# A graph attention layer: weighing ahead of the logits' transposes, and an older pair of blocks scaled ahead of the scans

## The chip, the cores and the metric

One core of a Trainium2 chip runs the kernel. The metric is the device time of one launch in microseconds (us). The profile is one execution recorded by the hardware profiler. Engines: PE is TensorE (matmuls, transposes), DVE is VectorE, ACT is ScalarE, POOL is GpSimd, SP is SyncE, which here only issues DMAs.

## The reference

There are 12,500 nodes with 256 features and 200,000 edges (src, dst), sorted by dst; 8 heads of 32.

```
h = relu(layernorm(x))
q, k, v = h @ Wq + bq, h @ Wk + bk, h @ Wv + bv          # 8 heads of 32
logits = einsum('ehd,ehd->eh', q[dst], k[src]) / sqrt(32)
expv = exp(logits - segment_max(logits, dst)[dst])
attn = expv / segment_sum(expv, dst)[dst]
agg = segment_sum(attn[:, :, None] * v[src], dst)
y = h + gelu(agg + h @ Wskip + bskip)
out = x + layernorm(y) * gamma + beta
```

## The kernel before

A first part makes the tables: h, k and v side by side (`kv_tab`), and q. A second part plans the walk over the edges. Both end near 395 us in the profile. The rest is the walk, and the change lies in it.

The edges are cut into 8 streams of 25,000. A step takes 383 edges of every stream, as K = 3 tiles of 128 edges; there are NST = 66 steps. The loop body numbered c holds work of several steps, and `keep` ties every instruction to the one before it on its own engine, so each engine runs in the order in which the code names the calls.

Work of a tile j of step c:
- `gather` (L1033, POOL): 8 indirect DMAs, one per stream, fetch k and v of 128 edges each, 24 a step. Six `kv` buffers hold two steps of tiles. `gather_next` puts them in four parts of two among DVE's work: the first part waits until its buffer is free, the other three wait for the latest DVE instruction named ahead of them.
- `hot_e` (L1050 on PE, L1052 on ACT) makes `to_e`, which spreads q from nodes to edges; six products a step, three in the middle of the body and three near its end. `hot_n` makes `to_n`, which sums edges into nodes.
- `spread` (L1073, PE): q of each edge, two halves. `times` (L1082, DVE): q times k. `total` (L1089, DVE): sums over each head, the logits `L`.
- `turn` (L1097, PE): transposes `L` into the PSUM tile `turned`. `maxima` (L1108, L1109, L1111, DVE): two scans along the edges of a stream, which need all three tiles turned, and a subtraction. `exponent` (L1115, ACT), `turn_back` (L1124, PE) puts the weights into other columns of the same tile `turned`.
- `weigh` (L1139, DVE): weight times v, into `vw`. It reads `turned`. `add_up` (L1163, PE; L1175 and L1181, ACT; L1185, SP) sums into nodes and stores the sums to `table` in DRAM.

A pair of 128-node blocks whose sums are complete is finished along the way, 46 of them in the loop, at most one begun in a step. `Pair` has these calls: `fetch` (six loads at L837: sums, x, h of two blocks), `turn` (L850 PE, L853 ACT), `divisors`, `divide` (L842 to L856, DVE), `skip` (L863, L867, PE), `add` (L872, PE), `gelu` (L876, ACT), `stats` (L879 to L885, DVE), `root` (L889, ACT), `factors` (L893, L894, DVE), `normal` (L899, ACT), `shifted` (L906, L909, PE), `scale` (L913, L915, DVE), `store` (L920, two stores by SP). The buffers of a pair are used again by the second pair after it.

In the body of step c, `pair` was fetched at the end of the body before; it goes as far as `gelu`. `before` is the pair of the previous body: it goes from `stats` to `store`. `pair_next` is fetched behind that store. Every load and store of a pair, the loads of q (`windows`, L1025, eight), `penalties` (L1011), `prefetch` (L1005) and the eight table writes (L1185) stand in SP's one queue in the order of the code.

Of the kernel before, what the change touches and what calls it, by code (L numbers as in the profile page):

```python
# [48 lines left out]
K = 3  # L49
# [710 lines left out]
def walk_streams(tc, N, HID, NST, KL, many, ident, idx, d0_row, slot_row, near, near_n, e_tab, pen_tab, h_tab,  # L760
# [48 lines left out]
    class Pair:  # L809
# [36 lines left out]
        def turn(self):  # L846
            ps = self.ps_h()
            for b in range(2):
                for c in range(KC):
                    self.keep(nc.tensor.transpose(ps[:, b, c, :], self.h[:, b, c * P:(c + 1) * P],  # L850
                                                  ident))
            self.hT = self.pool.tile([P, 2, KC, P], F32, name="hT", bufs=1)
            self.keep(nc.scalar.copy(self.hT, ps))  # L853
# [99 lines left out]
    with ExitStack() as es:  # L953
# [35 lines left out]
        def tiles_of(c):  # L989
            return KL if c == NST - 1 else K  # L990
# [36 lines left out]
        def gather(c, j, slots=range(S), behind=None):  # L1027

            if slots[0] == 0:
                step[c].setdefault("kv", []).append(gath.tile([P, S, KV], F32, name="kv"))  # L1030
            t = step[c]["kv"][j]
            for s in slots:
                ins = keep(nc.gpsimd.indirect_dma_start(  # L1033
                    out=t[:, s, :], out_offset=None, in_=kv_tab[:, :],
                    in_offset=bass.IndirectOffsetOnAxis(ap=idx[:, s, j, c:c + 1], axis=0)))
                if behind and s == slots[0]:
                    tc.add_manual_dep(ins.ins, behind, mybir.DependencyInfo(
                        mybir.DependencyClass.Sync, mybir.DependencyReason.DATA), reason="pace")

        def gather_next(c, j, part):  # L1040

            if 0 <= c < NST - 2 and j < tiles_of(c + 2):
                gather(c + 2, j, range(2 * part, 2 * part + 2), latest[DVE] if part else None)
# [22 lines left out]
        def spread(c, j, half):  # L1066

            g = step[c]
            ps = qe_ps.tile([P, 2, 2, HID], F32, name="ps_qe")
            for a in range(2):  # L1070
                for b in range(2):
                    i, at, w = rows_of(4 * half + 2 * a + b)
                    keep(nc.tensor.matmul(ps[:, b, a, :],  # L1073
                                          g["to_e"][at:at + w, i, j * P:(j + 1) * P],
                                          g["qw"][at:at + w, i, :], start=True, stop=True))
            g["qe", half] = ps
# [8 lines left out]
        def total(c, j):  # L1085
            g = step[c]
            if j == 0:
                g["L"] = work.tile([P, K, SH], F32, name="L")
            keep(nc.vector.tensor_reduce(g["L"][:, j, :].rearrange("p (s h) -> p s h", s=S),  # L1089
                                         g["kv"][j][:, :, :HID].rearrange(  # L1090
                                             "p s (h d) -> p s h d", h=HEADS),
                                         AX.X, OP.add))
# [9 lines left out]
        def maxima(c):  # L1102
            g = step[c]
            n = tiles_of(c) * P
            X, R, pen = turned[:SH, :n], turned[SH:, :n], g["pen"]
            M = g["M"] = work.tile([SH, CH], F32, name="M")[:, :n]
            W = g["W"] = work.tile([SH, CH], F32, name="W", bufs=1)[:, :n]
            keep(nc.vector.tensor_tensor_scan(R, pen[:SH, :n], X, -BIG, op0=OP.add, op1=OP.max))  # L1108
            keep(nc.vector.tensor_tensor_scan(mirrored(M, 0, n), mirrored(pen[SH:, :], 1, n),  # L1109
                                              mirrored(R, 0, n), -BIG, op0=OP.add, op1=OP.max))  # L1110
            keep(nc.vector.tensor_tensor(W, X, M, op=OP.subtract))  # L1111
# [23 lines left out]
        def weigh(c, j):  # L1135
            g = step[c]
            t = g["vw"][j]
            wj = weight(j)
            keep(nc.vector.tensor_tensor(  # L1139
                t[:, :, HEADS:].rearrange("p s (h d) -> p s h d", h=HEADS),  # L1140
                wj[:, :, :, None].to_broadcast([P, S, HEADS, D]),
                g["kv"][j][:, :, HID:].rearrange("p s (h d) -> p s h d", h=HEADS), op=OP.mult))
            if j == 0:
                keep(nc.vector.tensor_tensor(t[:, :, :HEADS], wj, wden[c % 2], op=OP.mult))  # L1144
# [96 lines left out]
                                  bank(i), keep))  # L1241
                lasts[i].fetch_rows()

        pair = before = None
        for c in range(NST - 1):

            pair_next = None
            if c in due:
                pair_next = Pair(fin, due[c][0],
                                 lambda: hot_ps.tile([P, 2, KC, P], F32, name="ps_hot"),  # L1250
                                 lambda: ag_ps.tile([P, 2 * HID], F32, name="ps_a").rearrange(
                                     "p (b d) -> p b d", b=2),
                                 keep)
            if c + 2 < NST:
                windows(c + 2)
            for half in range(2):
                times(c, K - 1, half)
                gather_next(c - 1, 1, 1 + half)
                spread(c + 1, 0, half)
            total(c, K - 1)  # L1260
            gather_next(c - 1, 1, 3)
            turn(c, K - 1)
            if c:
                weigh(c - 1, K - 1)
                gather_next(c - 1, K - 1, 0)
            maxima(c)
            gather_next(c - 1, K - 1, 1)
            if before:
                before.stats()
            if c:  # L1270
                add_up(c - 1, 0, range(K - 1, K))
                add_up_products(c - 1, 1)
            exponent(c)
            turn_back(c)
            if c:
                add_up_results(c - 1, 1)
            if c:
                add_up(c - 1, 2)
            carried(c)
            for half in range(2):  # L1280
                times(c + 1, 0, half)
                gather_next(c - 1, K - 1, 2 + half)
                spread(c + 1, 1, half)
            total(c + 1, 0)
            weigh(c, 0)
            gather_next(c, 0, 0)
            for j in range(K):
                hot_n(c, j)
            turn(c + 1, 0)
            if before:  # L1290
                before.root()
            if pair:
                pair.turn()
                pair.divisors()
                pair.divide()
                pair.skip()
            if before:
                before.factors()
            if c + 2 < NST:
                for i in range(QT // 2):  # L1300
                    hot_e(c + 2, i)
            if before:
                before.normal()
            if pair:
                table_of(AF.Gelu)
                pair.add()
                pair.gelu()
            if pair or before:
                table_of(AF.Exp)
            for half in range(2):  # L1310
                times(c + 1, 1, half)
                gather_next(c, 0, 1 + half)
                if tiles_of(c + 1) == K:
                    spread(c + 1, K - 1, half)
            total(c + 1, 1)
            gather_next(c, 0, 3)
            turn(c + 1, 1)
            if before:
                before.shifted()
            weigh(c, 1)  # L1320
            gather_next(c, 1, 0)
            if before:
                before.scale()
                before.store(0)
                before.store(1)
            if pair_next:
                pair_next.fetch()
            if c == NST - 2:
                for i in range(4):
                    last(i)  # L1330
            if c + 2 < NST:
                for i in range(QT // 2, QT):
                    hot_e(c + 2, i)
            add_up(c, 0, range(K - 1))
            if c + 2 < NST:
                penalties(c + 2)
            if c + 3 < NST:
                prefetch(c + 3)
            if c == NST - 2:
                weigh(c, K - 1)  # L1340
                add_up(c, 0, range(K - 1, K))
                add_up(c, 1)
                if pair_next:
                    pair_next.turn()
                    pair_next.skip()
            if c == NST - 2:
                add_up(c, 2)
            before, pair = pair, pair_next
            if c > 1:
                step[c - 2] = None  # L1350

        c = NST - 1
# [432 lines left out]
```

## Time and profile before

| | |
|---|---|
| median of 3 runs | 2546.08 us (2539.39 to 2546.2) |
| the profiled execution | 2542.74 us, span 2540.9 us |
| mean granted TensorE clock | 0.707 |
| busy: PE, DVE, ACT, POOL | 1772.4, 1998.0, 1081.4, 1659.9 us |
| DMA | 649.36 MB, mean 256 GB/s over the span |
| gathers by POOL (L1033) | 1576, 966 ns each |
| weigh on DVE (L1139) | 197, 2289 ns each |
| times (L1082), total (L1089) on DVE | 394 of 1217 ns, 197 of 2286 ns |

A row of the timeline has the start in us from the span's start, the duration, the engine, the line, the operation, output <- inputs, the shapes, the count, and in brackets the engine's idle time ahead of it with what ended it. A row of the list of waits has who waited, for whom, the total in us, how often, and the longest. "SPq" rows are SyncE's issues.

### The profile page before, as it was taken

How to read it: one execution, taken by the hardware profiler on the slowest of the kernel's cores; microseconds unless marked ns; L12 is line 12 of the kernel's file. 1: busy time of each engine (PE TensorE's matmuls, PEld its weight loads, DVE VectorE, ACT ScalarE, POOL GpSimd, SP SyncE). 2: the span in 40 equal slices, each digit the busy share in tenths (PEclk: the TensorE clock that was granted, in tenths of full speed). 3: DMA queues.
4: the chain of work that ended last, by engine and by line, in shares of the span. 5: the costliest groups of instructions: out<-in, count | busy, mean ns of one | idle time of the engine just before them, and what ended most of it. 6: DMA issues, size and time to landing. Idle time of an engine off the chain costs nothing. (4 is left out here: it accounts for less than half of the span.)

```text
span 2540.9 us, 29615 instructions
## 1 busy us (share of the span) xinstructions
PE 1772.4 (70%) x7824; PEld 926.5 (36%) x7824; DVE 1998.0 (79%) x2330; ACT 1081.4 (43%) x2459; POOL 1659.9 (65%) x1745
## 2 busy tenths in 40 slices
PE   6889974555567767667677677667777677676665
PEld 3445532222233333333333333333333333333333
DVE  7775946777788888888888888887877887888884
ACT  3333322333334545444444544444444444444443
POOL 3442447777777777677777677776776776776730
PEclk9999985666666766766676766676666766667677
DMA  7766678888898898888898898898887988988952
GB/s 249 272 227 248 256 256 247 255 260 258 254 278 256 270 281 254 267 276 260 252 279 272 252 280 265 262 278 256 264 267 242 290 253 244 293 255 257 291 169 79
DMA packets 306130, 649.36 MB, mean 256 GB/s; under 512 B 52836, under 2 KB 192238, under 8 KB 300954
## 3 DMA queue, kind: packets, MB, share of 16 engines
q0 software_dynamic: 128768, 423.23, 54.7%
q1 hardware_dynamic: 176434, 223.46, 26.7%
q8 instruction: 65, 1.06, 0.2%
q10 hardware_dynamic: 748, 0.66, 0.1%
q14 instruction: 115, 0.94, 0.1%
HBM read 538.91 MB, written 108.23 MB: 255 GB/s over the span
## 5 line engine op out<-in xcount | busy, mean ns | idle before, releaser
L1033 POOL DMA_INDIRECT kv<-kv_tab,idx x1576 | 1523.1, 966 | 567.9 <-issue 385.0
L1139 DVE TENSOR_TENSOR vw<-ps_x,kv 128x2048 f32<-128x2048 f32 x197 | 450.9, 2289 | 246.2 <-PE ps_x L1097 219.1
L1082 DVE TENSOR_TENSOR kv<-ps_qe,kv 128x1024 f32<-128x1024 f32 x394 | 465.4, 1217 | 84.0 <-DMA kv<-kv_tab,idx 82.0
L1089 DVE TENSOR_REDUCE L<-kv 128x64 f32<-128x2048 f32 x197 | 450.3, 2286 | 6.9 <-DVE kv L1082 0.2
L1163 PE MATMUL ps_a<-vw,to_n 128*32 128x264 f32 (+1 forms) x2344 | 304.5, 549 | 158.4 <-DVE vw L1139 158.4
L1073 PE MATMUL ps_qe<-qw,to_e 64*128 64x256 f32 (+1 forms) x1576 | 316.8, 400 | 111.2 <-DVE kv L1082 63.8
L1052 ACT ACTIVATE to_e<-ps_hot,ones 128x384 fp32r<-128x384 f32 x396 | 214.0, 576 | 364.1 <-PE ps_hot L1050 357.8
L1073 PEld LDWEIGHTS ps_qe<-qw,to_e 64*128 64x128 f32 (+1 forms) x1576 | 227.7, 253 | 281.6 <-DVE kv L1082 134.7
L1175 ACT COPY sums_w<-ps_a 128x264 f32<-128x264 f32 x130 | 49.3, 379 | 609.4 <-PE ps_a L1163 427.2
L1050 PE MATMUL ps_hot<-et,near 48*128 48x384 bf16 x396 | 150.6, 426 | 114.9 <-ACT to_e L1052 104.9
L1097 PE MATMUL ps_x<-ident,L 128*64 128x128 f32 x197 | 71.5, 363 | 210.6 <-DVE vw L1144 132.7
L1163 PEld LDWEIGHTS ps_a<-vw,to_n 128*32 128x32 f32 (+1 forms) x2344 | 103.2, 147 | 311.8 <-DVE vw L1139 189.1
L257 PE MATMUL ps_kv<-w_kv,hT 128*128 128x512 f32 x392 | 195.5, 621 | 16.0 <-ACT hT L142 14.8
L867 PE MATMUL ps_a<-w_s,hT 128*128 128x256 f32 x368 | 170.6, 644 | 50.3 <-ACT hT L853 49.6
L269 POOL TENSOR_TENSOR qp<-qp 128x256 fp32r<-128x256 f32 x98 | 88.4, 903 | 170.1 <-ACT qp L268 169.8
L1163 PE MATMUL ps_hot<-vw,to_n 128*64 128x264 f32 x808 | 187.6, 633 | 0.0
L867 PEld LDWEIGHTS ps_a<-w_s,hT 128*128 128x128 f32 x368 | 115.1, 328 | 94.4 <-ACT hT L853 69.6
L1181 ACT COPY kv<-ps_a 1x264 f32<-1x264 f32 x388 | 142.9, 368 | 6.3
L1097 PEld LDWEIGHTS ps_x<-ident,L 128*64 128x64 f32 x197 | 23.9, 121 | 310.3 <-DVE vw L1144 215.7
L987 ACT ACT_TABLE_LOAD x102 | 130.9, 1283 | 1.8
L1163 PEld LDWEIGHTS ps_hot<-vw,to_n 128*64 128x64 f32 x808 | 82.5, 219 | 109.2 <-issue 107.9
L263 PE MATMUL ps_q<-w_q,hT 128*128 128x256 f32 x392 | 104.1, 388 | 20.4 <-DVE qp L267 20.3
(278 smaller groups left out, 2110.3 us busy)
## 6 DMA issues: line engine op xcount, KB each, us to landing
qw<-q_pc SPq DMA_DIRECT2D x264, 128.0 KB
kv<-kv_tab,idx POOLq DMA_INDIRECT x1576
kv_tab<-kvo SPq DMA_DIRECT2D x16, 1280.0 KB
q_pc<-qp SPq DMA_DIRECT2D x16, 1280.0 KB
qw<-q_pc SPq DMA_DIRECT2D x264, 64.0 KB
table<-sums_w SPq DMA_DIRECT2D x264, 61.9 KB
pen<-pen_tab SPq DMA_DIRECT2D x66, 192.5 KB
sums<-table SPq DMA_DIRECT2D x92, 132.0 KB
```

The source lines that it names most:

```text
L257: ins = nc.tensor.matmul(ps_kv, hT[:, c, :], w_kv[:, c, :], start=c == 0, stop=c == KC - 1)
L867: self.keep(nc.tensor.matmul(self.ps[:, b, :], self.hT[:, b, c, :], w_s[:, c, :], start=False, stop=False, skip_group_check=True))
L987: keep(nc.scalar.activation(dummy[:, 1:2], dummy[:, 0:1], function))
L1033: ins = keep(nc.gpsimd.indirect_dma_start(out=t[:, s, :], out_offset=None, in_=kv_tab[:, :], in_offset=bass.IndirectOffsetOnAxis(ap=idx[:, ...
L1050: keep(nc.tensor.matmul(ps[:, :CH], near[:, i * P:(i + 1) * P], step[c]["et"], start=True, stop=True))
L1052: keep(nc.scalar.activation(step[c]["to_e"][:, i, :], ps[:, :CH], AF.Relu, scale=-1.0, bias=ones))
L1073: keep(nc.tensor.matmul(ps[:, b, a, :], g["to_e"][at:at + w, i, j * P:(j + 1) * P], g["qw"][at:at + w, i, :], start=True, stop=True))
L1082: keep(nc.vector.tensor_tensor(k, g["qe", half].rearrange("p b a d -> p a b d"), k, op=OP.mult))
L1089: keep(nc.vector.tensor_reduce(g["L"][:, j, :].rearrange("p (s h) -> p s h", s=S), g["kv"][j][:, :, :HID].rearrange("p s (h d) -> p s h d" ...
L1139: keep(nc.vector.tensor_tensor(t[:, :, HEADS:].rearrange("p s (h d) -> p s h d", h=HEADS), wj[:, :, :, None].to_broadcast([P, S, HEADS, D] ...
L1163: keep(nc.tensor.matmul(ps[at:at + w, :], g["to_n"][:, j, i * P + at:i * P + at + w], g["vw"][j][:, s, :], start=j == 0, stop=j == tiles_o ...
L1181: keep(nc.scalar.copy(step[c + 1]["kv"][0][0:1, s, HID - HEADS:], ps[at:at + 1, :]))
```

## The change

In the walk's loop: `weigh` of a tile stands directly behind the `total` of another tile, and the `turn` of that total behind it, at both places where it was the other way round. A pair is given a further body: `older` is the pair that was `before` a body earlier. `factors` and `normal` of `before` move behind the second `total`; `shifted`, `scale` and the two stores move into the next body, to `older`, `shifted` ahead of the first `total`, the others ahead of `maxima`. `fetch` moves from the end of a body to the next body, behind those stores. The last body does both at its end as before.

```diff
-        pair = before = None
+        pair = before = older = None
         for c in range(NST - 1):
...
                 times(c, K - 1, half)
                 gather_next(c - 1, 1, 1 + half)
                 spread(c + 1, 0, half)
+            if older:
+                older.shifted()
             total(c, K - 1)
             gather_next(c - 1, 1, 3)
-            turn(c, K - 1)
             if c:
                 weigh(c - 1, K - 1)
                 gather_next(c - 1, K - 1, 0)
+            turn(c, K - 1)
+            if older:
+                older.scale()
+                older.store(0)
+                older.store(1)
+            if pair:
+                pair.fetch()
             maxima(c)
...
                 pair.skip()
-            if before:
-                before.factors()
             if c + 2 < NST:
                 for i in range(QT // 2):
                     hot_e(c + 2, i)
-            if before:
-                before.normal()
             if pair:
                 table_of(AF.Gelu)
                 pair.add()
...
             total(c + 1, 1)
             gather_next(c, 0, 3)
+            if before:
+                before.factors()
+            weigh(c, 1)
+            gather_next(c, 1, 0)
             turn(c + 1, 1)
             if before:
-                before.shifted()
-            weigh(c, 1)
-            gather_next(c, 1, 0)
-            if before:
-                before.scale()
-                before.store(0)
-                before.store(1)
-            if pair_next:
-                pair_next.fetch()
+                before.normal()
             if c == NST - 2:
+                if before:
+                    before.shifted()
+                    before.scale()
+                    before.store(0)
+                    before.store(1)
+                if pair_next:
+                    pair_next.fetch()
                 for i in range(4):
                     last(i)
...
-            before, pair = pair, pair_next
+            older, before, pair = before if c < NST - 2 else None, pair, pair_next
```

## The prediction

> **What bounds the kernel now.** I read the list of waits first, because VectorE (DVE) has the largest share of the span (79%).
>
> ```profile
> DVE vw L1139 <- PE ps_x L1097: 219.1, 128, 5.4
> DVE rstd L893 <- ACT rstd L889: 65.0, 45, 2.9
> DVE kv L1082 <- DMA kv<-kv_tab,idx: 82.0, 30, 11.0
> POOL kv L1033 <- issue: 385.0, 1263, 0.3
> POOL kv L1033 <- DVE vw L1139: 75.5, 46, 3.4
> SPq L920 <- DMA out_dram<-o: 125.3, 48, 3.8
> ```
>
> Columns: total us, times, longest. DVE's largest wait is weigh (L1139) for a transpose of logits (L1097, turn). GpSimd's gathers mostly wait 0.3 us each, which is their own spacing.
>
> Next the timeline of one step, forward scan (L1108) to forward scan. DVE:
>
> ```profile
> 1535.61 0.96 DVE L1108 TENSOR_TENSOR_SCAN ps_x<-pen,ps_x 64x384 f32<-64x384 f32 x1
> 1546.53 0.21 DVE L1144 TENSOR_TENSOR vw<-ps_x,wden 128x64 f32<-128x64 f32 x1
> 1548.98 0.17 DVE L893 RECIPROCAL rstd<-rstd 128x2 f32<-128x2 f32 x1 [1.14 <-ACT rstd L889]
> 1551.78 2.29 DVE L1089 TENSOR_REDUCE L<-kv 128x64 f32<-128x2048 f32 x1
> 1558.96 2.29 DVE L1139 TENSOR_TENSOR vw<-ps_x,kv 128x2048 f32<-128x2048 f32 x1 [4.90 <-PE ps_x L1097]
> 1567.75 2.29 DVE L1139 TENSOR_TENSOR vw<-ps_x,kv 128x2048 f32<-128x2048 f32 x1 [0.52 <-PE ps_x L1097]
> ```
>
> TensorE (PE) in the same stretch:
>
> ```profile
> 1549.47 3.78 PE L867 MATMUL ps_a<-w_s,hT 128*128 128x256 f32 x8 [1.61 <-ACT hT L853]
> 1554.76 2.07 PE L872 MATMUL ps_a<-o,ident 128*128 128x256 f32 x4
> 1556.76 1.95 PE L1073 MATMUL ps_qe<-qw,to_e 64*128 64x256 f32 x8
> 1558.51 0.41 PE L1097 MATMUL ps_x<-ident,L 128*64 128x128 f32 x1
> 1559.39 2.08 PE L909 MATMUL ps_hot<-x_f,ident 128*128 128x256 f32 x4
> ```
>
> The transpose that weigh waits for is late because PE is late: it stands behind skip (L867), three to_e products, add (L872) and spread (L1073). So removing DVE's wait exposes PE next. SyncE:
>
> ```profile
> 1528.21 3.64 SPq L920 DMA_DIRECT2D out_dram<-o  x2
> 1532.51 0.35 SPq L837 DMA_DIRECT2D sums<-table  x1
> 1535.50 0.38 SPq L837 DMA_DIRECT2D h<-h_tab  x1
> ```
>
> The second store waits until the first has landed, and the fetch comes behind both.
>
> The scans' start times give step lengths. Steps 2 to 10, without pairs, average 30.3 us and wait some 5 us each for gathers. Steps 12 to 63 take 1684 us, 32.4 each. By content: 24 steps A (a pair computed, an earlier one finished, an older one to come; 19 of about 34.4, 5 of 32.4), 10 B (no older pair yet; nine of 32.2, one of 34.6), 9 C (no pair computed; 30.6), 9 D (a pair computed, none in normalisation; five of 30.5, four of 29.0). The clock separates the long and the short ones: the windows show PE granted 0.50 from 1548 to 1575, where the eight spread products take 1.95 us, and 1.00 from 1521 to 1527, where they take 1.17.
>
> **GpSimd's floor.** A gather takes 966 ns (page) plus 385.0/1263 = 0.305 us spacing; 24 per step make 30.5 us. No step can be shorter on average. Steps 0 to 10 stand there already, so I count nothing for them, nor for the first 395 us and the tail behind step 64, whose order is nearly the same.
>
> **Part by part, for step A**, in us from the scan start, 1535.61 as zero.
> - Weigh ahead of turn: takes away 4.90 + 0.52 of DVE wait. The transposes now stand behind weigh: 0.31 to start plus 0.42. The first is waited for only a step later; the second stands ahead of the scans, where the two scaling operations (0.68 + 0.69) cover 0.73. Without an older pair it costs that 0.73.
> - Factors later: the 1.14 wait (2.35 in C) goes, since the root ends at 13.3 and factors now come at about 17. The two normal activations (1.08) move behind ACT's Gelu and Exp loads, ahead of the last three to_e reliefs: PE's sixth to_e product waits for them.
> - Shifted, scale and stores one step later: as many instructions. Shifted (0.60 + 2.08, or 0.38 + 1.13 at full clock) now stands in PE behind spread, ahead of the last transpose, and scale's second half needs it.
> - Fetch: same six DMAs, but in the step that uses them. On SyncE they move from ahead of pen, et and the eight window loads to behind the two stores and ahead of the eight table writes. The first table write now waits for both sums to land, with half a step to spare. The window loads no longer queue behind the stores; they start when PE has done the last spread and take 6.59, so SyncE is free about 1 (full clock) to 3 us (half) before the stores.
>
> When do rows land? From the end of scale: last h issued at +7.3 (1535.50 - 1528.19). In the trace's release times h lands 6.03 after its issue (median of 26; 5.06 to 8.01), sums 5.58 (5.22 to 6.15). The store's landing is 3.16 in the median (1.72 to 4.72). So h lands between 10.9 and 16.9; I take 14.0, a little above the medians' 13.3, because window loads now stand just ahead in SyncE's queue. Sums land near 12.5, DVE wants them at 11.06 (A) or 9.4 (D): it waits 1.5 to 3, but PE's chain hides that. For h, hT is copied at 14.5 to 15.05 instead of 13.24 to 13.80: 1.25 late, the rest hidden by ACT's root.
>
> The Trainium skill, "DMA: Bandwidth & Descriptors", section "Anatomy of one DMA", gives, fitted for transfers that GpSimd issues, about 2.0 us plus bytes/436e3, an estimate of 2.3 us for these 128 KB; the trace has 6.03. By the rule nothing would be late and the sum would fall to the GpSimd floor.
>
> Chain of A at half clock: hT 15.05; skip, to_e and add end 7.4 later (as now, 13.80 to 21.2): 22.45; Gelu 0.57, Exp load and dummy 1.5, normal 1.08, relief 0.58: 26.2; sixth product 0.4, sums 1.99, spread 1.95, shifted 2.68, scale 0.69: 34.0. DVE alone would be there at 31. So **34.1** against 34.4: nearly all of the 5.4 reappears behind PE. At full clock (rows of the step at 1503: 5.94 from hT to add; 0.57, 1.48, 1.08, 0.56; 0.33, some 1.2, 1.17, 1.51, 0.69) PE ends at 29.6 and DVE at **29.9**, against 32.4.
> B has its rows early (no store before them): 1.25 less, and no more than that: 32.8 or 28.6. C loses 2.35 and 1.5 and gets the scaling it has today: 27.0 to 28.5, I take 27.5. D gains nothing at ACT, pays the late rows and 0.73 ahead of the scans: 31.3 or 29.1, a little worse than now.
>
> Sum with each step's clock as it is now: 19 x 34.1 + 5 x 29.9 + 9 x 28.6 + 32.8 + 9 x 27.5 + 5 x 31.3 + 4 x 29.1 = 1608. C, D, B in a row would ask their gathers in 28.4 to 29.1 each, under the floor by 4 to 6 us per group, of which the six kv buffers lend most: I add 10 for nine groups. 1684 - 1618 = 66 us. The profiled execution took 2542.7 (span 2540.9 and 1.8 around it; 3.3 under the median of the runs): **2477**, I say 2475. About 0.3%, 7.6 us, is what a measurement can tell from no change.
>
> **The clock.** The Trainium skill, "TensorE: Matmul & The Clock Gate", Part 1, says the clock halves after an idle window of about 3.4 us and returns after a busy one. The rows have 0.50 for 27 us in which PE's longest idle is 2.4, so the measurement decides. By the rule alone most steps would run at full clock, near 2445; but a wait for h beyond 15 would itself make a 3.4 us gap, which speaks against the change.
>
> **Rivals.**
> 1. GpSimd becomes the bound: PE gets warmer because its 2.38 us gap before the last sums goes. 52 x 30.5 = 1586: 98 less, 2445. For: the POOL row; against: half clock in most pair steps.
> 2. The rows come too late. Place: h for PE's transposes (L850) in the 33 steps A and D, each 1:1. Every us beyond 14.0 costs 33; at 2.0 beyond (16.0) the gain is gone; at 17 to 18 it is 2576 to 2609. For: landing rows to 8.01, window loads close ahead of the stores; half clock in B and C as well (10 x 4 and 9 x 1) does the same. Against: medians.
> 3. PE's own order gives everything back (A and B at half clock throughout, C as taken, rows on time): 24 x 34.1 + 10 x 32.8 + 9 x 27.5 + 9 x 31.3 = 1676, with the 10 no change: 2543 to 2546.
>
> **Chances.** Forecast (2455 to 2500) 0.45; rival 1 0.20; rival 2 0.25; rival 3 0.10, of which 0.03 falls on the faster side and 0.01 on the slower. Faster 0.68, same 0.06, slower 0.26. Range 2437 to 2557: from rival 1's end to the beginning of rival 2.
>
> **What the profile after would show.** Right: L1139's wait for L1097 under 20 us; L893's wait near nothing; new waits of L842 for sums and of L850 for h of 1 to 3 us in A and D; L915 waiting for PE; L1050 waiting longer for ACT; C under 29, A at half clock near 34. Wrong: waits for h over 4 us (rival 2), or GpSimd with hardly any wait but its 0.3 (rival 1).

## The result and the profile after

The changed kernel takes 2443.9 us (median of 4 runs, 2443.03 to 2448.57), the kernel before 2546.14 beside it: a ratio of 0.961, 95% interval 0.959 to 0.963. The profiled execution has a span of 2441.2 and takes 2443.03, 99.7 less than that of before. By the scans' start times, 97.5 of this lie in the 52 steps 12 to 63 (1684.3 before, 1586.8 after), 1.4 ahead of the first scan, 1.1 in steps 0 to 11; behind step 64 it is 0.3 longer.

The list of waits of the whole execution, after:

```profile
POOL kv L1033 <- issue: 357.8, 1174, 0.3
PE ps_x L1097 <- DVE vw L1139: 118.9, 57, 3.8
DVE kv L1082 <- DMA kv<-kv_tab,idx: 131.5, 64, 11.6
DVE kv L1082 <- PE ps_qe L1073: 77.0, 38, 3.5
DVE o L915 <- PE ps_hot L909: 47.8, 26, 3.5
PE ps_hot L850 <- DMA h<-h_tab: 37.0, 36, 2.5
DVE den L842 <- DMA sums<-table: 26.7, 29, 2.5
```

The wait of weigh (L1139) for the transposes (L1097), 219.1 us before, is gone from the list; now the transposes wait for weigh. The wait of factors for the root (L893, 65.0) is down to 2.8. New are waits for a pair's rows (L842, L850) and for its scaling product (L915), and VectorE's wait for gathered rows is longer than before (131.5 against 82.0).

The list of waits again, GpSimd alone, in the walk's 52 steps only. Before (759 to 2443.6):

```profile
POOL kv L1033 <- DVE vw L1139: 74.3, 42, 3.4
POOL kv L1033 <- DVE kv L1082: 44.0, 74, 2.4
```

After (757 to 2344):

```profile
POOL kv L1033 <- issue: 283.2, 929, 0.3
POOL kv L1033 <- DMA kv<-kv_tab,idx: 35.0, 115, 0.3
POOL kv L1033 <- DVE vw L1139: 5.8, 19, 0.3
```

The last column is what counts. Before, GpSimd stood up to 3.4 us for buffers that VectorE had not freed; over the steps 85 us lay beyond its own spacing. After, not one gather waits longer than 0.3, whoever is named: GpSimd issues without a break. Its cadence (the time from one gather's start to the next) is 0.965 + 0.305 = 1.27 us there, and 52 x 24 x 1.27 = 1585; the steps take 1586.8.

A view by windows has, for each stretch, each engine's busy time with the instructions in brackets, the clock, the DMA share and GB/s. The 52 steps after:

```profile
757.00:2344.00 1587.00, 1130.80 (x5482) 593.54 (x5476) 1374.93 (x1349) 798.30 (x1749) 1206.03 (x1250) 0.72 0.89 281
```

Before, the same stretch of work took 1684 with a granted clock of 0.67. By kinds of step:

| | forecast | measured (least to most) | clock before, after |
|---|---|---|---|
| A, 24 steps | 34.1 (19 of them), 29.9 (5) | 31.5 (30.3 to 33.7) | 0.67, 0.73 |
| B, 10 | 32.8 (1), 28.6 (9) | 31.7 (30.3 to 32.7) | 0.71, 0.73 |
| C, 9 | 27.5 | 27.8 (26.3 to 30.8) | 0.61, 0.66 |
| D, 9 | 31.3 (5), 29.1 (4) | 29.3 (27.7 to 31.4) | 0.70, 0.73 |

The longest step A after begins its scan at 1368.67 and takes 33.74. VectorE:

```profile
1386.69 2.29 DVE L1139 TENSOR_TENSOR vw<-ps_x,kv 128x2048 f32<-128x2048 f32 x1
1392.08 2.37 DVE L1082 TENSOR_TENSOR kv<-ps_qe,kv 128x1024 f32<-128x1024 f32 x2 [3.11 <-PE ps_qe L1073]
1401.81 0.69 DVE L915 TENSOR_TENSOR o<-sums,ps_hot 128x512 f32<-128x512 f32 x1 [2.25 <-PE ps_hot L909]
```

TensorE and GpSimd in it:

```profile
1382.59 0.69 PE L850 MATMUL ps_hot<-ident,h 128*128 128x128 f32 x2 [1.54 <-DMA h<-h_tab]
1383.95 3.78 PE L867 MATMUL ps_a<-w_s,hT 128*128 128x256 f32 x8
1391.24 1.94 PE L1073 MATMUL ps_qe<-qw,to_e 64*128 64x256 f32 x8
1399.70 2.08 PE L909 MATMUL ps_hot<-x_f,ident 128*128 128x256 f32 x4
```

```profile
1385.56 0.95 POOL L1033 DMA_INDIRECT kv<-kv_tab,idx  x1 [0.30 <-issue]
1389.34 0.95 POOL L1033 DMA_INDIRECT kv<-kv_tab,idx  x1 [0.30 <-DVE vw L1139]
```

Weigh no longer waits, and its 4.90 us have gone to TensorE as forecast: 3.11 at the next times, because skip (L867, 3.78 at half clock) holds the spread back, and 2.25 at the scaling. The last h lands 13.8 behind the end of the previous scaling (1382.59 - 1368.76). So this step is the forecast's A at half clock, 33.7 against 34.1. But GpSimd goes on through it at its cadence, into buffers freed earlier, and the short steps behind it catch up: the next one, a C, takes 27.2.

### The profile page after: what moved, and what is told of

It is laid out like the page before. It is cut to its first block, busy times and chain, and to the rows that moved or that the text cites. A ratio compares the mean times of both kernels' runs of the same rounds, so it can differ in the third digit from the quotient of the medians.

```text
span 2441.2 us, 29592 instructions
## 1 busy us (share of the span) xinstructions
PE 1707.4 (70%) x7824; PEld 908.6 (37%) x7824; DVE 1983.1 (81%) x2330; ACT 1086.9 (45%) x2459; POOL 1654.2 (68%) x1745
## 3 DMA queue, kind: packets, MB, share of 16 engines
q1 hardware_dynamic: 176434, 223.46, 27.2%
## 4 chain that ended last, share of the span: by engine, by line
PE 24%; DMA 23%; DVE 19%; issue 12%; POOL 11%; ACT 7%; SPq 2%; DVEq 0%; another core or an unknown queue 0%; ACTq 0%; POOLq 0%
DMA kv<-kv_tab,idx 15%; POOL kv L1033 10%; DVE vw L1139 5%; PE ps_a L867 5%; PE ps_kv L257 5%; DVE kv L1082 5%; DMA h<-h_tab 4%; DVE L L1089 3%; PE ps_q L263 3%; PE ps_qe L1073 3%; DMA out_dram<-o 2%; PE ps_a L1163 2%; ACT L987 2%; PE ps_a L872 2%; PE ps_hot L1050 1%
## 5 line engine op out<-in xcount | busy, mean ns | idle before, releaser
L1082 DVE TENSOR_TENSOR kv<-ps_qe,kv 128x1024 f32<-128x1024 f32 x394 | 469.0, 1218 | 213.3 <-DMA kv<-kv_tab,idx 131.5
L1139 DVE TENSOR_TENSOR vw<-ps_x,kv 128x2048 f32<-128x2048 f32 x197 | 449.5, 2282 | 15.4 <-ACT vw L1133 15.4
L1073 PE MATMUL ps_qe<-qw,to_e 64*128 64x256 f32 (+1 forms) x1576 | 313.4, 397 | 101.8 <-DVE kv L1082 98.2
L1073 PEld LDWEIGHTS ps_qe<-qw,to_e 64*128 64x128 f32 (+1 forms) x1576 | 224.8, 250 | 268.6 <-DVE kv L1082 156.6
L1163 PE MATMUL ps_a<-vw,to_n 128*32 128x264 f32 (+1 forms) x2344 | 283.1, 511 | 3.3 <-DVE vw L1139 3.3
L1097 PE MATMUL ps_x<-ident,L 128*64 128x128 f32 x197 | 73.4, 373 | 270.4 <-DVE vw L1144 145.2
L1050 PE MATMUL ps_hot<-et,near 48*128 48x384 bf16 x396 | 145.2, 427 | 126.2 <-ACT to_e L1052 121.7
L867 PE MATMUL ps_a<-w_s,hT 128*128 128x256 f32 x368 | 172.7, 649 | 20.9 <-ACT hT L853 17.5
L1163 PEld LDWEIGHTS ps_a<-vw,to_n 128*32 128x32 f32 (+1 forms) x2344 | 101.7, 140 | 202.9 <-issue 165.1
L1097 PEld LDWEIGHTS ps_x<-ident,L 128*64 128x64 f32 x197 | 25.1, 127 | 365.7 <-DVE vw L1144 221.3
L1163 PE MATMUL ps_hot<-vw,to_n 128*64 128x264 f32 x808 | 141.8, 500 | 0.9 <-DVE o L915 0.6
L867 PEld LDWEIGHTS ps_a<-w_s,hT 128*128 128x128 f32 x368 | 115.5, 329 | 69.3 <-ACT hT L853 44.2
L1063 ACT ACTIVATE to_n<-ps_hot,ones 128x384 f32<-128x384 f32 x197 | 104.0, 582 | 31.8 <-PE ps_hot L1061 31.0
```

What stands on the lines that cost most here:

```text
L867: self.keep(nc.tensor.matmul(self.ps[:, b, :], self.hT[:, b, c, :], w_s[:, c, :], start=False, stop=False, skip_group_check=True))
L1050: keep(nc.tensor.matmul(ps[:, :CH], near[:, i * P:(i + 1) * P], step[c]["et"], start=True, stop=True))
L1073: keep(nc.tensor.matmul(ps[:, b, a, :], g["to_e"][at:at + w, i, j * P:(j + 1) * P], g["qw"][at:at + w, i, :], start=True, stop=True))
L1082: keep(nc.vector.tensor_tensor(k, g["qe", half].rearrange("p b a d -> p a b d"), k, op=OP.mult))
L1139: keep(nc.vector.tensor_tensor(t[:, :, HEADS:].rearrange("p s (h d) -> p s h d", h=HEADS), wj[:, :, :, None].to_broadcast([P, S, HEADS, D] ...
L1163: keep(nc.tensor.matmul(ps[at:at + w, :], g["to_n"][:, j, i * P + at:i * P + at + w], g["vw"][j][:, s, :], start=j == 0, stop=j == tiles_o ...
```

## The experiments

**Theory:** in the changed kernel's walk GpSimd's issuing of gathers ends last, 30.5 us a step, and the swap of weigh and turn is what brought the other engines under it. **Rivals:** the pair's move did it; late rows of the pair still cost; transfers, or the chain of VectorE and TensorE, end at 30.5 by coincidence.

The runs fell on several chips. On one the kernel before takes 2541 us, nearly as in the first comparison; on three others it takes 3165, 3165 and 3214. There TensorE stands still at times with no releaser in the record, which is not explained, and ratios alone are compared.

**The changed kernel again**, no edit (on the chip with 2541).

> The changed kernel once more, on the chip of these runs, so that the others have it beside them. Where the kernel before takes 2546 us, both theories expect 2444. On a chip as in the runs before this one, where it takes about 3165 us because TensorE stands still with no releaser in the record: weighing ahead of the turn alone was worth a ratio of 0.964 there and the pair's move alone 0.9935, so their sum is 0.958; the theory of GpSimd's floor (30.5 us a step) expects between 0.955 and 0.965, as steps of 40 us do not touch that floor. The rival, that the pair's move is what mattered, expects that the two together are far below 0.95.

2447.84 us (2444.19 to 2449.32), ratio 0.963 [0.961, 0.965]. The 52 steps take 1590.8, again without a gather of GpSimd that waits longer than 0.3.

**h fetched early** (same chip).

```diff
-                self.rows_of(self.h[:, b, :], h_b, rows[b], HID)
+        def fetch_h(self):
+            self.h = self.pool.tile([P, 2, HID], F32, name="h")
+            rows = loaded(slot_row[0:1, self.m, 0:2], (N - P) * BX)
+            for b in range(2):
+                self.rows_of(self.h[:, b, :], h_b, rows[b], HID)
...
                 if pair_next:
                     pair_next.fetch()
+            if pair_next:
+                pair_next.fetch_h()
```

> The changed kernel, but the loads of h are issued at the end of the body before, where all six loads of a pair stood in the kernel before; sums and x stay at the new place. Theory of GpSimd's floor: h's wait (81 us in the trace of after, over PE and its weight loads) lies under the floor; where the kernel before takes 2546 us the time is that of the changed kernel, 2444, within 0.3 percent. Rival, late rows are what is left of the cost: 33 steps get up to 2.9 us each back, so 2444 less 40 to 80. On a chip where the kernel before takes 3165: in the trace there h was waited for 1 us in all, so no change beside the changed kernel.

2452.66 us (2450.79 to 2454.53), against 2447.84 for the changed kernel beside it: not faster by 40 to 80, but 5 slower (0.2%). The list of waits (lines stand 4 lower in this kernel: L846 is L842, L854 is L850, L1086 is L1082):

```profile
DVE den L846 <- DMA sums<-table: 9.9, 13, 1.6
PE ps_hot L854 <- DMA h<-h_tab: 1.8, 1, 1.8
DVE kv L1086 <- DMA kv<-kv_tab,idx: 179.3, 76, 11.2
POOL kv L1037 <- issue: 326.9, 1072, 0.3
```

Against the trace of the changed kernel beside it, the waits for h fell from 35.2 to 1.8 on TensorE and for sums from 29.6 to 9.9 on VectorE, and VectorE waits 179.3 instead of 137.9 for gathered rows: what the pair no longer waits for is waited for at the gathers. Steps D even grew (30.6 against 29.1 in the run beside it) and A shrank (31.1 against 31.6), with the 52 steps at 1595.8. So three executions of two orders, with different lengths of their kinds of step, end between 1587 and 1596. Even these 9 us are GpSimd's: over the 52 steps a gather took 965.3 ns in the mean in the first trace, 968.5 in the second and 971.7 here, with 304.9 ahead of it in each, and the 1249, 1249 and 1250 gathers so make 1586.4, 1590.4 and 1595.8 us, where the steps take 1586.8, 1590.8 and 1595.8. The rival of late rows falls.

**Two gathers fewer a step, in the kernel before** (same chip).

```diff
             for s in slots:
+                if c > 1 and j == K - 1 and s % 4 == 3:
+                    keep(nc.sync.dma_start(t[:, s, :], kv_tab[s * P:(s + 1) * P, :]))
+                    continue
                 ins = keep(nc.gpsimd.indirect_dma_start(
```

> The kernel before with two of a step's 24 gathers (third tile, streams 3 and 7, from step 2) replaced by plain loads of 128 neighbouring rows through SyncE; these rows are other rows than the reference's. It takes 2.5 us of GpSimd's time out of each step. Theory: the kernel before is bound by the chain of VectorE and TensorE and touches GpSimd's floor only in part (85 us of GpSimd's idle beyond its spacing lie in the loop), so where it takes 2546 us it gets 0 to 60 us less, where the changed kernel would get some 100 less. On a chip where it takes 3165: a ratio of 0.98 to 1.0, against 0.921 for the same edit of the changed kernel. Rival, that transfers (and not GpSimd's issues) are the bound: then the gain is nothing in both, as the same bytes are fetched.

2517.4 us, ratio 0.991 [0.989, 0.993]. Windows of steps 0 to 11 and of the 52 steps, first the kernel before, then with fewer gathers:

```profile
395.00:759.00 364.00, 200.74 (x1030) 96.07 (x1029) 280.26 (x195) 115.75 (x295) 275.59 (x291) 0.62 0.85 258
759.00:2443.00 1684.00, 1192.35 (x5470) 613.10 (x5470) 1387.00 (x1349) 793.20 (x1748) 1216.24 (x1255) 0.67 0.87 265
```

```profile
393.00:733.00 340.00, 201.16 (x1030) 95.83 (x1029) 279.61 (x195) 115.68 (x295) 257.55 (x271) 0.62 0.89 279
733.00:2417.00 1684.00, 1186.18 (x5470) 610.96 (x5470) 1386.88 (x1349) 793.55 (x1748) 1105.20 (x1148) 0.68 0.85 265
```

This is the clearest reading of the study. In steps 0 to 11 GpSimd has no wait beyond 0.3 in either kernel; twenty gathers less took 24 us off there (20 x 1.27 = 25.4), though as many bytes were moved (the plain loads read neighbouring rows), and GB/s rose from 258 to 279. So neither the transfers nor the other engines set that stretch, GpSimd's issuing did. In the 52 steps GpSimd did 111 us less and the time did not move: its waits for VectorE took it up, and weigh's wait for the transposes stayed (201.2, before 203.0).

```profile
POOL kv L1036 <- DVE vw L1142: 103.2, 50, 3.7
POOL kv L1036 <- DVE kv L1085: 99.5, 104, 3.7
```

(Of these 52 steps; L1142 is weigh, L1085 times.) The kernel before was bound there by the chain of VectorE and TensorE; the kernel after shows in these steps the state that before shows only in steps 0 to 11.

**The swap alone**, twice, on chips where the kernel before takes 3165 and 3214. The edit, in the kernel before, at the first place (the second alike):

```diff
-            turn(c, K - 1)
             if c:
                 weigh(c - 1, K - 1)
                 gather_next(c - 1, K - 1, 0)
+            turn(c, K - 1)
```

> Before, with weigh ahead of turn at both places and nothing else moved: the pair keeps its three bodies. Theory 1 (the loop now goes by GpSimd's gathers, 24 x 1.27 = 30.5 us a step; the swap brings it near there, the pair's move the rest): the 203 us of waits at L1139 in steps 12 to 63 vanish, the 61 us for the root at L893 stay, the scans (L1108) get a new wait of about 0.5 to 0.7 us in every step (25 to 35 us in all), and A comes to 31 to 32.5: 2455 to 2490 us in all. Theory 2 (it was the pair's move that freed DVE, the swap only trades one wait for another): 2525 or more.

3049.64 us against 3164.84: 0.964 [0.961, 0.967].

> The kernel before with weigh ahead of turn at both places, the pair's calls where they were; once more, as the runs before were on a chip where the kernel before takes 3165 us and the last ones on one where it takes 2541. Where it takes 2541: the theory says that the swap takes nearly all of VectorE's wait of 219 us for the transposes and brings most steps to GpSimd's floor of 30.5 us, 2450 to 2480, ratio 0.965 to 0.976. Rival, that the pair's move opens the way (without it TensorE's and ScalarE's order in the pair steps gives the gain back): 2510 to 2541.

3099.45 against 3213.68: 0.965 [0.963, 0.967]. The microseconds expected for a chip with 2541 could not be tested.

**The pair's move alone**, the changed kernel with turn ahead of weigh, on the same two chips.

```diff
+            turn(c, K - 1)
             if c:
                 weigh(c - 1, K - 1)
                 gather_next(c - 1, K - 1, 0)
-            turn(c, K - 1)
```

> After, with turn ahead of weigh again at both places; the pair's fourth body, the late factors and the late fetch stay. Theory 1: the waits at L1139 stay at 200 us or more, and the rows that land late put PE further behind: 2545 to 2590 us, no gain or a loss. Theory 2 (the pair's move gives the gain): 2490 or less.

> The changed kernel with turn ahead of weigh again, so that the pair's move is alone. Where the kernel before takes 2541: the theory says 2510 to 2541, since VectorE's wait of 5 us for the transposes in each pair step stays and only the wait of factors for the root (65 us) goes, most of which the wait for the transposes takes up. Rival, that the pair's move is what mattered: 2450 to 2480.

0.9935 [0.9905, 0.9966] (3148.47 against 3164.84) and 0.9983 [0.9965, 1.0001] (3206.06 against 3213.68). The lists of waits of the second runs, the swap alone and then the pair's move alone:

```profile
DVE rstd L893 <- ACT rstd L889: 77.7, 42, 5.3
DVE ps_x L1108 <- remote: 230.9, 27, 14.3
```

```profile
DVE rstd L893 <- ACT rstd L889: 7.5, 2, 4.7
DVE vw L1139 <- PE ps_x L1097: 191.8, 37, 14.1
```

("remote" is a wait whose releaser the record does not have.) With the swap alone weigh's wait for the transposes is not in the list and the wait for the root is still there; with the pair's move alone it is the other way round, and the time hardly moves. So on those chips the swap alone brings a ratio of 0.964 to 0.965, the pair's move alone at most 1%. The changed kernel did not run there without a further edit, so what the two give together on those chips is not measured; with the memsets below it took 0.961 and 0.964. The rival of the pair's move falls there. That the shares are the same on the chip of the comparison was not tested, and the waits are not the same: with the swap alone weigh still waits 260.9 us for ScalarE (L1133) in the second run, where that wait is 15.4 in the first trace of the changed kernel.

**More and less of GpSimd's work in the changed kernel.** Four memsets in each body, and the two gathers fewer as above. All of these runs, and the one with memsets in the kernel before, fell on the slower chips.

```diff
+        idle = one.tile([P, 80], F32, name="idle")
...
                 windows(c + 2)
+            for _ in range(4):
+                keep(nc.gpsimd.memset(idle, 0.0))
```

> After, with four small memsets on GpSimd in every body (they take its time and move no data). Theory 1 (GpSimd is saturated from the first gather to the last): all of the added time, busy plus spacing as the rows of this run show it, comes out of the span: 65 bodies times it, within 15%. Theory 3 (DMA bandwidth or PE and DVE bound the loop at the same 30.5 by chance): a third of it or less.

> The changed kernel with four memsets of 128x80 float32 on GpSimd in each body, into a tile that nothing reads. Each takes 0.17 us and 0.04 ahead of it by the earlier trace, 0.85 a body, 44 in the 52 steps and 55 in 65 bodies. Theory, that GpSimd's issuing is the bound of the changed kernel's walk: 2444 plus 44 to 60, so 2488 to 2505. Rival, that the chain of VectorE and TensorE, or the transfers, happen to end at 30.5: 2444 to 2460.

> Before, with the same four memsets in every body. Theory 1: GpSimd has 85 us of slack in steps 12 to 63, so only steps 0 to 11 pay in full (12 times the added time) and the others little, as long as the added time stays under 1.6 us a step. Were GpSimd the bound of the kernel before as well, it would pay 65 times.

> After, with two of the 24 gathers of every step (the third tile's streams 3 and 7, from step 2 on) replaced by plain loads of as many bytes on SyncE's queue; they bring other rows, so those edges carry wrong keys and values. GpSimd's floor falls from 24 to 22 gathers, 27.9 us a step; DMA bytes stay. On a chip where the kernel before takes some 2546 us: theory 1 (GpSimd is the bound of the loop after): steps 12 to 63 lose at least the 39 us that DVE waits there for gathers and at most 52 x 2.5 = 132, steps 0 to 11 some 25 to 30: 2290 to 2385 us. Theory 3 (DMA bandwidth binds, or PE's chain of the forecast, 1608 us for those 52 steps): 2420 or more.

> The changed kernel with two of a step's 24 gathers (third tile, streams 3 and 7, from step 2) replaced by plain loads of 128 neighbouring rows through SyncE; these rows are other rows than the reference's, the bytes are as many. GpSimd's floor falls from 30.5 to 27.9 a step. The same edit of the kernel before took 24 us, all in steps 0 to 12, and nothing in the 52 steps behind (1684.5 against 1684.3). Theory: here those 52 steps fall too, from 1587 to between 1500 and 1560, where the chain of VectorE and TensorE ends; with the 24 of the first steps 2330 to 2395. Rival, that something else ends at 30.5 (the transfers, or that chain): only the 24, 2420.

With memsets: 3042.36 against 3164.84 (one run), and 0.964 [0.959, 0.969] (3094.26 against 3213.68); in the kernel before 3139.70 (one run), below its 3164.84 without them. With fewer gathers: 0.921 [0.914, 0.927] (2913.12) and 0.916 [0.913, 0.919] (2939.72). The list of waits of the first run with fewer gathers:

```profile
POOL kv L1036 <- DVE W L1114: 394.3, 62, 8.9
PE ps_hot L1053 <- issue: 222.2, 100, 8.6
```

GpSimd has 408 to 526 us of idle beyond its spacing ahead of the gathers of the 52 steps in these four runs of the changed kernel (0.2 in its first trace), so these runs can't say what added or removed time does where it has none: for the question they were made for they are inconclusive. Between the swap alone and fewer gathers the 52 steps fall from 2115.9 to 1977.4 us (the second runs), 2.7 a step, about the 2.5 that GpSimd was spared, although it has idle time and although the two kernels also differ by the pair's move; this is not explained.

## Why the prediction was right and wrong

**Right:** the direction, and the time lies in the range. That it does is owed to the range being drawn out to rival 1's end; the sum of the parts, 2475, is 31 us too long, and for it the hit is luck. The order's working held: weigh's wait went and TensorE took up much of it (in the 52 steps VectorE waits 73.3 us for the spread, L1073, and 47.8 for L909, where it had waited 203.0 for the transposes); L893's wait went; L1050 waits longer for ScalarE (121.7, before 104.9); C takes 27.8 in the mean where 27.5 was taken, though singly 26.3 to 30.8; A at half clock takes 33.7 where 34.1 was.

**What came was rival 1,** with a chance of 0.20, to the microsecond in the loop: 52 x 30.5 = 1586 forecast, 1586.8 measured, and 2445 against 2443.9. The sign named for it, GpSimd with hardly any wait but its 0.3, is what the profile shows. The likeliest case, 2475 within 2455 to 2500, did not come. The steps that failed:

- "Sum with each step's clock as it is now". Nineteen steps A were priced at half clock, 34.1. After, 3 of 24 are at 33 or more and 10 at 30.8 or less, and the clock of A rose from 0.67 to 0.73. (The terms listed for that chain add up to 33.9, not 34.0, and 34.1 went into the sum; in 19 steps this is under 4 us.) A is 42 us below its term (24 x 31.5 = 756 against 797), D 9 below, C 3 above and B 27 above. The last is no error of the chain's working that could be read off: once GpSimd sets the pace, a step's length is no longer the end of its chain.
- "I add 10 for nine groups". GpSimd's floor was handled as a correction to the chain's sum. The forecast 1608 stood only 22 above the floor; a fall of the chain by more than that could only give 1586. The floor should have been one arm of a maximum, with the chance set by how certain those 22 were. The 10 came to nothing: with six buffers, long and short steps evened out fully.
- "I take 14.0" for the last h. It lands 12.6 behind the end of scale in the median of 32 (11.2 to 14.6), and its own landing is 5.3 where 6.03 was taken from the trace of before. Sums land at about 11, not near 12.5; L842's waits are 0.9 each, not 1.5 to 3. Rival 2 (over 16) was never near. The rows' estimate so made the chain too long in A and D, by 1.4 us at most; by the experiment with h, what is left of these waits costs nothing under the floor. The rule of the Trainium skill, "DMA: Bandwidth & Descriptors", section "Anatomy of one DMA", fitted for transfers that GpSimd issues, erred further on the other side for these of SyncE: an estimate of 2.3 us by it, 5.3 in the trace.

Why TensorE's clock rose is not shown. Rival 1 put it down to TensorE's wait for weigh ahead of the last sums (L1163 for L1139), and this fell from 158 to 3 us. But the new waits of the transposes for weigh (118.9) are no smaller singly: 2.1 each and up to 3.8, where the waits ahead of the sums had been 2.3 each and up to 2.9. TensorE stands idle for 29% of the 52 steps in both traces.

The Trainium skill's rule on the clock ("TensorE: Matmul & The Clock Gate", Part 1) would, by the prediction's estimate, also have given about 2445, but the trace does not bear it out. Windows of the step at 1368:

```profile
1385.00:1395.00 10.00, 8.84 (x26) 4.86 (x24) 6.82 (x7) 6.65 (x12) 7.56 (x9) 0.50 0.85 262
1395.00:1402.40 7.40, 7.40 (x39) 3.68 (x38) 5.15 (x4) 0.95 (x2) 5.57 (x7) 0.50 0.93 303
```

TensorE is busy for 16.24 of these 17.4 us, in the last 7.4 without a break, and the granted clock stays at 0.50 to the end of them, where the rule has it return after a busy window of about 3.4. By the clock's records it returns at 1402.8, some 7.9 us after TensorE's last pause. These records change at multiples of 3.41 us. In the 52 steps of both traces each return to 1.00 (90 before, 87 after) follows a stretch of 3.41 us in which TensorE was at least 83% busy, and each fall to 0.50 (90 and 86) one in which it was at most 70% busy, though in the kernel before its longest pause was 2.7 us. That does not tell why the clock was higher in the changed kernel: many full stretches at 0.50 are followed by another at 0.50.

**Open:** what the chain alone would take in the changed kernel. VectorE still waits 39.5 us for gathered rows in the 52 steps, so it probably lies not far below the floor; the runs with fewer gathers, which would show it, were on other chips. Open too: why the clock rose, and what the swap alone gives on the chip of the comparison.

## What to carry to other kernels

When one engine has a fixed cadence per step, write the forecast as the larger of that cadence and the chain's end, summed over the loop, and ask first whether the chain's sum is further above the cadence than its own error. The longest entry of that engine's wait list tells which side holds: only its own spacing (here 0.3) means that it sets the pace, and then a wait seen on another engine, such as the one for h here, is no longer worth anything. Where a read and a write of different columns of one PSUM tile meet, as in weigh and turn, look at the order of the two on their engines: here turning it round alone was worth a ratio of 0.964 and 0.965, the move of the pair's work alone 0.994 and 0.998 (on the slower chips).

## What the runs showed of the hardware

- GpSimd's indirect gathers of 128 rows kept a cadence of 1.27 us (0.965 and 0.305) in the comparison's trace, and when two of 24 a step were replaced by plain loads, steps 2 to 9 of the kernel before fell from 30.2 to 27.7 us each, while DMA carried more per second (279 against 258 GB/s over steps 0 to 11).
- The kernel before took 24 to 26% longer on three other chips. The durations of single gathers are the same there (0.96 us), but TensorE has 221 to 574 us of idle without a recorded releaser, against 40 (before) and 0 (after) in the first comparison. Gathers wait for VectorE there (394.3 us for L1114 alone in the first run with fewer gathers) and VectorE has waits without a recorded releaser, so which is the cause stays open.
- A fall of TensorE's granted clock to 0.50 needed no long pause: in the kernel before it fell 90 times in the 52 steps, where TensorE's longest pause was 2.7 us.
